# Two-layer graph kernel: short products gathered into blocks of two graphs, on five shared single PSUM banks

## The chip, the cores and the metric

The kernel runs on one core of one Trainium2 chip. The metric is the device time of one launch in microseconds (us), from the first to the last instruction of that core. Inputs and outputs lie in the chip's main memory, all in 32-bit floats.

A core has a tensor engine (PE, matrix products; its weight loads are listed as PEld), a vector engine (DVE), a scalar engine (ACT), GpSimd (POOL), and a queue engine (SP) that issues transfers (DMA). PE writes its results into PSUM, a small memory that is handed out in banks of 512 floats for each of 128 partitions; DVE and ACT read them from there.

## What is computed

There are 128 graphs of 128 nodes with 512 features each, and one adjacency matrix for all. Two layers follow each other, each with a residual sum and a normalization over the features:

```python
def layer0(x, adj, Wq, Wk, Wv):
    q, k, v = x @ Wq.T, x @ Wk.T, x @ Wv.T              # for each graph
    rel = adj.T * (q @ k.T)
    rel = rel / norm(rel, over the last axis)
    return rel @ v

def layer1(x, adj, Wq, bq, Wk, bk, Wv, bv):              # 8 heads of 64
    q, k, v = x @ Wq + bq, x @ Wk + bk, x @ Wv + bv      # split into heads
    scores = q @ k.T / sqrt(64) + where(adj == 0, -1e9, 0)
    return softmax(scores) @ v                           # heads side by side

x = layernorm(x + layer0(x, adj, ...))
x = layernorm(x + layer1(x, adj, ...))
```

## The kernel before

The graphs are worked on in 32 groups of four (`g`), with `b` the graph within its group. Layer 0 uses one folded matrix `m` for q and k. The five large products (m, v0, q, k, v1) are each done on four graphs at once, with seven half-size products in place of eight. Each of the seven is a dense step: 8 matmul instructions of 256 columns.

```python
def product(self, i, bank, start):
    ...
    for m in range(2):
        for k in range(2):
            nc.tensor.matmul(bank[:, m, :], l[:, k, m * P:(m + 1) * P], r[:, k, :], ...)

def step(self, i):
    if i == 1:
        self.begin()
        self.a = ps_a.tile([P, 2, HF], F32, tag="a", ...)
        self.product(1, self.a, True)
        self.empty(self.s[:, 0], self.a, 0)          # ACT empties the partial sum
    elif i == 5:
        self.b = ps_b.tile([P, 2, HF], F32, tag="b", ...)
        ...
    elif i == 2:
        d = ps_b.tile([P, 2, HF], F32, tag="d", ...)
        self.product(2, d, True)
        self.add(0, 0, d, 0)                         # DVE adds and empties
    elif i == 6:
        self.product(6, self.a, False)               # adds on to what is in the bank
        self.empty(self.s[:, 2], self.a, 0)
    # ... 3 and 7 add on to b and a and are added by DVE, 4 is emptied by ACT
```

Everything else is short work. The program of every engine is written by hand, by a table of positions. `at(r, k, f, ...)` puts a piece of short work into round `r` ahead of dense step `k`; a round has 35 positions, and a position over 35 falls into the next round. Halves give only a finer order: 10.5 and 11 both stand between the dense steps 10 and 11.

```python
R = 35
def at(r, k, f, *a):
    short.setdefault(R * r + k, []).append((f, a))

for r in range(-1, NG):
    todo = [("m", r + 1), ("v0", r + 1)] if r < NG - 1 else []
    ...
    todo += [("q", r), ("k", r), ("v1", r)]
    for j, (kind, g) in enumerate(todo):
        ...
        for k, i in ((0, 1), (1, 5), (3, 6), (4, 2), (5, 3), (6, 7), (9, 4)):
            dense[R * r + 7 * j + k] = (pr, i)
```

The short work on PE that matters here:

```python
def l0_score(g, b):                      # scores of layer 0, whole array
    p = ps_m.tile([P, P], F32, tag="m", name=f"pst_{g}_{b}")
    ...
def l0_norm(g):                          # sums of squares: 128 rows, 32 columns of the array
    pn = ps_m.tile([P, G, Q], F32, tag="m", name=f"pn_{g}")
    for q in range(A):
        nc.tensor.matmul(pn[q * Q:(q + 1) * Q], ones, sq[:, :, q * Q:(q + 1) * Q], ...)
    nc.vector.transpose(ss, pn)
    ...
def l0_out(g, b):                        # rel @ v of layer 0, whole array
    p = ps_m.tile([P, D], F32, tag="m", name=f"po0_{g}_{b}")
    ...
def attn_scores(g, b):                   # 8 heads, two side by side on 64 rows each
    p = ps_s.tile([P, 2, A, H // 2, Q], F32, tag="s", name=f"ps_{g}_{b}")
    for a in range(H // 2):
        for s in range(2):
            r = slice(s * HD, (s + 1) * HD)
            nc.tensor.matmul(p[:, s, :, a, :], QT[g][r, a, b, :], KT[g][r, a, b, :], start=True, stop=True)
    w = two.tile(...)
    nc.vector.scalar_tensor_tensor(w..., p..., HD ** -0.5, mask..., op0=ALU.mult, op1=ALU.add)
def attn_out(g, b):                      # 8 heads, two side by side on 64 columns each
    p = ps_m.tile([P, H // 2, P], F32, tag="m", name=f"po1_{g}_{b}")
    for a in range(H // 2):
        for s in range(2):
            h = 2 * a + s
            nc.tensor.matmul(p[s * HD:(s + 1) * HD, a, :], V1[g][:, b, h * HD:(h + 1) * HD],
                             wT[:, s * (H // 2) + a].rearrange("p q t -> p (q t)"), start=True, stop=True)
    oT = one.tile(...)
    nc.vector.transpose(oT..., p...)
    ...
```

Between the scores and the product with v of one graph stand the row maximum (DVE), eight exponentials (ACT), a write to main memory and back in another order (`attn_spill`, `attn_stage`), and a transpose in blocks of 32 (`attn_transpose`, DVE). After the product its transpose goes out and back once more (`attn_back`, `attn_rows`). `attn_sum` divides by the softmax's sums and adds bias and residual, and `attn_stats`, `attn_norm` and `attn_write` finish the graph.

The PSUM pools before, in banks: `ps_a` 2, `ps_b` 2 (tags b and d), `ps_s` 2 (one tile of two banks), `ps_m` 2.

Of the kernel before, what the change touches and what calls it, by code (L numbers as in the profile page):

```python
# [8 lines left out]
F32 = mybir.dt.float32  # L9
# [9 lines left out]
def kernel(  # L19
# [15 lines left out]
    nc = tc.nc  # L35
# [14 lines left out]
    dram = ctx.enter_context(tc.tile_pool(name="dram", bufs=2, space=bass.MemoryType.DRAM))  # L50
    ps_a = ctx.enter_context(tc.tile_pool(name="ps_a", bufs=2, space=bass.MemoryType.PSUM))
    ps_b = ctx.enter_context(tc.tile_pool(name="ps_b", bufs=1, space=bass.MemoryType.PSUM))
    ps_s = ctx.enter_context(tc.tile_pool(name="ps_s", bufs=1, space=bass.MemoryType.PSUM))
    ps_m = ctx.enter_context(tc.tile_pool(name="ps_m", bufs=2, space=bass.MemoryType.PSUM))

    Q = 32
    A = P // Q
# [185 lines left out]
    class Projection:  # L243
# [56 lines left out]
# [3 lines that stand above are left out]
                self.a = ps_a.tile([P, 2, HF], F32, tag="a", name=f"pa_{self.name}")  # L303
                self.product(1, self.a, True)
                self.empty(self.s[:, 0], self.a, 0)
            elif i == 5:
                self.b = ps_b.tile([P, 2, HF], F32, tag="b", name=f"pb_{self.name}")
                self.product(5, self.b, True)
                self.empty(self.s[:, 1], self.b, 1)
            elif i == 2:  # L310
                d = ps_b.tile([P, 2, HF], F32, tag="d", name=f"pd_{self.name}")
                self.product(2, d, True)
                self.add(0, 0, d, 0)
            elif i == 6:
                self.product(6, self.a, False)
                self.empty(self.s[:, 2], self.a, 0)
            elif i == 3:
                self.product(3, self.b, False)
                self.add(0, 1, self.b, 2)
            elif i == 7:  # L320
                self.product(7, self.a, False)
                self.add(1, 1, self.a, 1)
            elif i == 4:
                self.product(4, self.a, False)
                self.empty(self.out(1, 0), self.a, 1)
# [65 lines left out]

    def attn_scores(g, b):

        p = ps_s.tile([P, 2, A, H // 2, Q], F32, tag="s", name=f"ps_{g}_{b}")
        for a in range(H // 2):
            for s in range(2):
                r = slice(s * HD, (s + 1) * HD)
                nc.tensor.matmul(p[:, s, :, a, :], QT[g][r, a, b, :], KT[g][r, a, b, :], start=True, stop=True)  # L398

        w = two.tile([P, 2, A, H // 2, Q], F32, tag="xl" if g == NG - 2 and b >= 2 else "w", name=f"w_{g}_{b}")  # L400
        nc.vector.scalar_tensor_tensor(w.rearrange("p s q a r -> p s (q a r)"),  # L401
                                       p.rearrange("p s q a r -> p s (q a r)"), HD ** -0.5,
                                       mask[:, None, :].to_broadcast([P, 2, D]), op0=ALU.mult, op1=ALU.add)
        nmax = small.tile([P, H], F32, tag="nmax", name=f"nmax_{g}_{b}")
        sums = small.tile([P, H], F32, tag="sums", name=f"sums_{g}_{b}")
        SOFT[g, b] = [w, nmax, sums]
# [26 lines left out]
            nc.sync.dma_start(wl[q * Q:(q + 1) * Q].rearrange("p a i r -> p a (i r)"), rows[:, :, q, :])  # L433

    def attn_transpose(g, b):
        wT = one.tile([P, H, A, Q], F32, tag="wT", name=f"wT_{g}_{b}")
        nc.vector.transpose(wT, SOFT[g, b][0].rearrange("p a i r -> p i a r"))  # L437
        SOFT[g, b][0] = wT

# [2 lines left out]
    def attn_out(g, b):  # L442
# [4 lines left out]
        for a in range(H // 2):  # L447
            for s in range(2):
                h = 2 * a + s
                nc.tensor.matmul(p[s * HD:(s + 1) * HD, a, :], V1[g][:, b, h * HD:(h + 1) * HD],  # L450
                                 wT[:, s * (H // 2) + a].rearrange("p q t -> p (q t)"), start=True, stop=True)
        oT = one.tile([P, A, H // 2, Q], F32, tag="oT", name=f"oT_{g}_{b}")
        nc.vector.transpose(oT.rearrange("p q a r -> p a q r"), p.rearrange("p a (q t) -> p a q t", t=Q))  # L453
        rs = small.tile([P, 2, 2, H // 2], F32, tag="rs", name=f"rs_{g}_{b}")
        nc.vector.reciprocal(rs, sums.rearrange("p (s a) -> p s a", s=2)[:, :, None, :].to_broadcast([P, 2, 2, H // 2]))
# [16 lines left out]
    def attn_sum(g, b):  # L472

        o, xr, rs = SOFT[g, b]
        f = o.rearrange("p f a r -> p (f a) r")
        nc.vector.tensor_tensor(f, f, rs.rearrange("p s y a -> p (s y a)")[:, :, None].to_broadcast([P, A * H // 2, Q]),  # L476
                                op=ALU.mult)
        nc.gpsimd.tensor_tensor(xr, xr, bv_b, op=ALU.add)  # L478
        nc.gpsimd.tensor_tensor(o, o, xr.rearrange("p (a f r) -> p f a r", a=H // 2, f=A), op=ALU.add)  # L479
        SOFT[g, b] = o  # L480

    def attn_stats(g, b):
        o = SOFT.pop((g, b))
        stats = small.tile([P, 1, 2], F32, tag="stats1", name=f"st1_{g}_{b}")
        statistics(o.rearrange("p f a r -> p (f a r)"), stats, 0, f"1_{g}_{b}")
        rstd = inverse_std(stats, 1, f"1_{g}_{b}")
        SOFT[g, b] = o, rstd, shift(stats, rstd, 1, f"1_{g}_{b}")

    def attn_norm(g, b):
        o, rstd, sh = SOFT.pop((g, b))  # L490
        y = two.tile([P, D], F32, tag="y", name=f"y_{g}_{b}")
        nc.scalar.activation(y.rearrange("p (a f r) -> p f a r", a=H // 2, f=A), o, AF.Identity,
                             bias=sh[:, 0:1], scale=rstd[:, 0:1])
        SOFT[g, b] = y

    def attn_write(g, b):
        nc.sync.dma_start(out[g * G + b], SOFT.pop((g, b)))

# [4 lines left out]
            nc.gpsimd.tensor_tensor(X[g, h], X[g, h], bv_b[:, None, :].to_broadcast([P, 2, D]), op=ALU.add)  # L505

    def last_scores(g, b):
        p = ps_s.tile([P, 2, H // 2, P], F32, tag="s", name=f"ps_{g}_{b}")
        for a in range(H // 2):
            for s in range(2):  # L510
                r = slice(s * HD, (s + 1) * HD)
                nc.tensor.matmul(p[:, s, a, :], QT[g][r, a, b, :], KT[g][r, a, b, :], start=True, stop=True)
        w = two.tile([P, H, P], F32, tag="w" if b < 2 else "xl", name=f"w_{g}_{b}")
        nc.vector.scalar_tensor_tensor(w, p.rearrange("p s a j -> p (s a) j"), HD ** -0.5,
                                       maskp[:, None, :].to_broadcast([P, H, P]), op0=ALU.mult, op1=ALU.add)
        nmax = small.tile([P, H], F32, tag="nmax", name=f"nmax_{g}_{b}")
        nc.vector.tensor_reduce(nmax, w, axis=AX.X, op=ALU.max, negate=True)
        sums = small.tile([P, H], F32, tag="sums", name=f"sums_{g}_{b}")
        SOFT[g, b] = w, nmax, sums, graph(g, b)
# [15 lines left out]
    def last_out(g, b, s):  # L535

        _, _, sums, xr = SOFT[g, b]
        if s == 0:
            LT["p", b] = ps_b.tile([P, H // 2, 2, HD], F32, tag="bd"[b % 2], name=f"po1_{g}_{b}")
            LT["rs", b] = small.tile([P, H], F32, tag="rs", name=f"rs_{g}_{b}")  # L540
        if b == 0 and s == 0:
            LT["o"] = one.tile([P, G, D], F32, tag="v1", name=f"o_{g}")
# [30 lines left out]
    def last_store(g, b):  # L573
# [6 lines left out]
    R = 35  # L580
    dense, short = {}, {}

    QUICK = (
        (32, (34, 34, 34, 35), (36, 38), 38, (43, 44, 45, 47, 51, 51, 55.5, 56.5)),
        (35, (37, 38, 39, 40), (38, 40), 40, (46, 48, 48, 50, 53, 54, 56, 60)),
        (38, (40, 40.5, 40.5, 41), (42, 43), 46, (48, 51, 51, 52.5, 56.5, 59.5, 62, 62.5)),
        (38.5, (43, 44, 45, 45), (45, 47), 49, (52, 53, 54, 56, 60, 63, 65, 66)),
    )
    LAST = (
        (17, (19, 20), (24, 24), (25.5, 27), 31, 33, 33),  # L590
        (17.5, (20.5, 21.5), (24, 24.5), (25.5, 27.5), 34.5, 34.5, 35),
        (19, (24, 25), (27, 27), (28.5, 31.5), 34.5, 35.5, 36),
        (20.5, (23.5, 27), (30.5, 31), (34, 35), 38.5, 39, 39),
    )

    def at(r, k, f, *a):
# [14 lines left out]
    for g in range(NG):  # L611

        for h in range(2):
# [2 lines left out]
                at(g - 1, 12 + 4 * h, load, g, h)  # L616
        last = g == NG - 1

        sc, no, ou, de, ln, sp, st, tr = (
            (18, 22, (36, 36, 37, 37), 38, 39, 40, (42, 43), (46, 47, 49, 50)) if g == 0 else  # L620
            (11, 16, (18, 19, 21, 22), 23, 24, 25, (26, 28), (31, 32, 33, 34)) if last else
            (11, 17, (19, 21, 23, 25), 26, 27, 29, (30, 32), (36, 37, 39, 40)))
        for h in range(2):
            at(g - 1, sp + h * (g in (0, NG - 1)), x1_spill, g, h)
            at(g - 1, st[h], x1_stage, g, h)
        for i, (dh, h) in enumerate(halves):
            at(g - 2, ((24, 25, 27, 28) if g != 1 else (22, 23, 24, 25))[i], x_transpose, g, dh, h)
            at(g - 1, tr[i], x1_transpose, g, dh, h)
        for b in range(G):
            at(g - 1, sc + b, l0_score, g, b)  # L630
            at(g - 1, ou[b], l0_out, g, b)
            at(g - 1, ln + b // 2, l0_layernorm, g, b)
        at(g - 1, no, l0_norm, g)
        at(g - 1, de, l0_rstd, g)

# [2 lines left out]
        for b in range(G):  # L638
            if last:
# [7 lines left out]
                at(g, no, last_norm, g, b)  # L647
                at(g, w, last_store, g, b)
                continue
            if g == NG - 2:  # L650
                s, ex, sp, st, pk = QUICK[b]
            else:
                s = (32, 39, 46, 52)[b]
                v = s + (14, 13, 14, 15)[b]
                ex, sp, st = (s + 2, s + 3, s + 4, s + 5), (s + 4, s + 6), s + 8
                pk = v - 2, v, v + 1, v + 3, v + 6, v + 9 + (b == 1), v + 11 + (b == 1), v + 13
            at(g, s, attn_scores, g, b)
            at(g, s + 1, attn_max, g, b)
            for i in range(4):
                at(g, ex[i], attn_exp, g, b, 2 * i)  # L660
            for i in range(2):
                at(g, sp[i], attn_spill, g, b, i)
            at(g, st, attn_stage, g, b)
# [48 lines left out]
```

## Time and profile before

| | before |
|---|---|
| time, median of 3 | 2519.33 us (2519.09 to 2522.44) |
| span of the profiled run | 2520.1 us |
| instructions | 41502 |
| matmul instructions on PE | 14656 |
| masked scaling of the scores (DVE, 128x1024) | 124, 1211 ns each |
| transpose of the product with v (DVE, 128x512) | 124, 715 ns each |
| exponentials (ACT, 128x128) | 992, 392 ns each |
| additions into o (POOL, 128x512) | 124, 1271 ns each |
| traffic with main memory | 159 GB/s over the span |

How it is read: for each engine the profile gives the busy time and its share of the span, and for each group of instructions the count, the mean length of one, and the idle time ahead of them with what ended it. Names are those of the program's tiles: `pa`, `pb` and `pd` are the banks of dense steps, `ps` the scores of layer 1, `po<-wT,v` its product with v, `po<-v,rel` the product of layer 0, `pst` the scores of layer 0, `pn` the sums of squares. The column such as `64*128` gives the rows and columns of the array that a matmul uses. In the list of waits a line tells who waited for whom, for how long in total, how often, and the longest. A chain of waits is followed back from the last instruction. A timeline merges neighbours of one kind and gives start, length and count.

### The profile page before, as it was taken

What the parts mean: (1) busy time and instruction counts of PE and PEld (TensorE: products, weight loads), DVE (VectorE), ACT (ScalarE), POOL (GpSimd) and SP (SyncE); (2) the same over time, 40 slices, a digit from 0 to 9 for tenths busy, and PEclk for the clock granted to TensorE, in tenths of its full rate; (3) what the DMA queues carried; (4) which work ended last, traced back from release to release, by engine and by line L of the source; (5) the groups of instructions that cost most, each with busy time, mean ns of one, the idle gap of its engine ahead of it and who ended that gap; (6) DMA issues with size and microseconds to landing.
All of it is one profiled execution on the core that took longest, in us unless ns stands there. A gap on an engine that the chain in (4) does not pass through costs nothing.

```text
span 2520.1 us, 41502 instructions
## 1 busy us (share of the span) xinstructions
PE 2498.5 (99%) x14656; PEld 2105.4 (84%) x14656; DVE 1559.6 (62%) x2587; ACT 1020.4 (40%) x3211; POOL 840.5 (33%) x1206
## 2 busy tenths in 40 slices
PE   8999999999999999999999999999999999999998
PEld 5888888888888888888888888888888888888886
DVE  5455666655666656666556666666665666665667
ACT  1234344434444443444344444444443444433445
POOL 3223333333333233332333332333323333323333
PEclk9999999999999999999999999999999999999999
DMA  7356556656566565565655665656656556656554
GB/s 156 101 135 179 144 165 182 164 153 170 145 183 172 150 172 146 169 180 158 161 163 152 180 174 152 169 145 177 172 148 180 151 159 182 169 153 169 147 166 134
DMA packets 508561, 404.74 MB, mean 161 GB/s; under 512 B 37568, under 2 KB 424768, under 8 KB 508352
## 3 DMA queue, kind: packets, MB, share of 16 engines
q1 hardware_dynamic: 508352, 402.08, 59.1%
q8 instruction: 115, 1.88, 0.3%
q14 instruction: 94, 0.77, 0.1%
HBM read 237.31 MB, written 164.63 MB: 159 GB/s over the span
## 4 chain that ended last, share of the span: by engine, by line
PE 98%; DVE 1%; DMA 1%; issue 0%; POOL 0%; SPq 0%; POOLq 0%; ACT 0%; DVEq 0%
PE pa_v L283 17%; PE pa_q L283 9%; PE pa_m L283 9%; PE pa_k L283 9%; PE pb_v L283 9%; PE ps L398 5%; PE po L450 5%; PE pst L335 5%; PE po L380 5%; PE pd_v L283 5%; PE pb_q L283 4%; PE pb_k L283 4%; PE pb_m L283 4%; PE pd_m L283 2%; PE pd_k L283 2%; PE pd_q L283 2%
## 5 line engine op out<-in xcount | busy, mean ns | idle before, releaser
L418 ACT ACTIVATE w<-w,nmax 128x128 f32<-128x128 f32 x992 | 385.6, 392 | 441.1 <-DVE nmax L411 412.9
L283 PE MATMUL pa_v<-wc_v,tx 128*128 128x256 f32 x1536 | 363.2, 379 | 0.4 <-DVE v L298 0.4
L283 PEld LDWEIGHTS pa_v<-wc_v,tx 128*128 128x128 f32 x1536 | 289.2, 190 | 38.8 <-DVE v L298 0.6
L453 DVE STREAM_TRANSPOSE oT<-po 128x512 f32<-128x512 f32 x124 | 88.7, 715 | 331.6 <-PE po L450 331.6
L360 POOL TENSOR_SCALAR ve<-st 128x1 f32<-128x1 f32 (+1 forms) x160 | 36.5, 228 | 628.7 <-DVE st L356 625.7
L478 POOL TENSOR_TENSOR xr<-xr,bv_b 128x512 f32<-128x512 f32 x124 | 159.2, 1284 | 234.7 <-DMA xr<-x1d 213.8
L479 POOL TENSOR_TENSOR o<-o,xr 128x512 f32<-128x512 f32 x124 | 157.6, 1271 | 147.1 <-DVE o L476 136.4
L401 DVE SCALAR_TENSOR_TENSOR w<-ps,mask 128x1024 f32<-128x1024 f32 x124 | 150.2, 1211 | 69.1 <-PE ps L398 68.9
L337 POOL TENSOR_TENSOR sq<-rel 128x128 f32<-128x128 f32 x128 | 51.1, 399 | 421.4 <-DVE rel L336 421.4
L476 DVE TENSOR_TENSOR o<-o,rs 128x512 f32<-128x512 f32 x124 | 89.0, 718 | 164.2 <-DMA o<-od 164.2
L418 ACT ACTIVATION_READ_ACCUMULATOR w<-w,nmax 128x1 f32 x992 | 188.4, 190 | 0.0
L283 PE MATMUL pa_q<-tx,wc_q 128*128 128x256 f32 x768 | 184.9, 383 | 0.0
L283 PE MATMUL pa_m<-tx,wc_m 128*128 128x256 f32 x768 | 181.5, 379 | 0.8 <-DVE yT L298 0.8
L283 PE MATMUL pa_k<-tx,wc_k 128*128 128x256 f32 x768 | 181.6, 379 | 0.0
L283 PEld LDWEIGHTS pa_q<-tx,wc_q 128*128 128x128 f32 x768 | 143.2, 190 | 37.3 <-issue 15.0
L294 ACT ACTIVATE s_q<-pa_q,bq_sb 128x256 f32<-128x256 f32 x128 | 53.6, 469 | 274.9 <-PE pa_q L283 273.5
L283 PEld LDWEIGHTS pa_m<-tx,wc_m 128*128 128x128 f32 x768 | 145.8, 190 | 21.4 <-DVE yT L298 1.2
L283 PEld LDWEIGHTS pa_k<-tx,wc_k 128*128 128x128 f32 x768 | 145.8, 190 | 20.1 <-issue 0.2
L411 DVE TENSOR_REDUCE nmax<-w 128x4 f32<-128x512 f32 x248 | 156.4, 672 | 0.1
L375 ACT ACTIVATE x<-x,sh,rstd 128x512 f32<-128x512 f32 x128 | 93.9, 804 | 153.3 <-POOL sh L370 153.3
L437 DVE STREAM_TRANSPOSE wT<-wl 128x1024 f32<-128x1024 f32 x124 | 153.1, 1235 | 0.6 <-DMA wl<-wd 0.4
L398 PE MATMUL ps<-kT,qT 64*128 64x128 f32 x1984 | 144.1, 285 | 0.0
(159 smaller groups left out, 5036.0 us busy)
## 6 DMA issues: line engine op xcount, KB each, us to landing
wd<-w SPq DMA_DIRECT2D x248, 256.0 KB, 2.6
wl<-wd SPq DMA_DIRECT2D x496, 128.0 KB, 3.0
xl_x<-in_x_dram SPq DMA_DIRECT2D x256, 128.0 KB, 6.7
x<-in_x_dram SPq DMA_DIRECT2D x64, 512.0 KB, 5.9
x1d<-x SPq DMA_DIRECT2D x64, 512.0 KB, 2.8
xl_h<-x1d SPq DMA_DIRECT2D x256, 128.0 KB, 3.5
od<-oT SPq DMA_DIRECT2D x496, 64.0 KB, 1.8
o<-od SPq DMA_DIRECT2D x124, 256.0 KB, 3.1
```

What stands on the lines that cost most here:

```text
L283: nc.tensor.matmul(bank[:, m, :], l[:, k, m * P:(m + 1) * P], r[:, k, :], start=start and m == 0 and k == 0, stop=(m == 1 and k == 1), ski ...
L335: nc.tensor.matmul(p, XT[g][:, dc, b, :], YT[g][:, dc, b, :], start=(dc == 0), stop=(dc == C - 1))
L375: nc.scalar.activation(h, h, AF.Identity, bias=sh[:, b:b + 1], scale=rstd[:, b:b + 1])
L380: nc.tensor.matmul(p, REL[g][0][:, b, :], V0[g][:, b, :], start=True, stop=True)
L398: nc.tensor.matmul(p[:, s, :, a, :], QT[g][r, a, b, :], KT[g][r, a, b, :], start=True, stop=True)
L401: nc.vector.scalar_tensor_tensor(w.rearrange("p s q a r -> p s (q a r)"), p.rearrange("p s q a r -> p s (q a r)"), HD ** -0.5, mask[:, Non ...
L411: nc.vector.tensor_reduce(nmax[:, s * (H // 2):(s + 1) * (H // 2)], w[:, s].rearrange("p q a r -> p a q r"), axis=AX.XY, op=ALU.max, negat ...
L418: nc.scalar.activation(w[:, s, :, a, :], w[:, s, :, a, :], AF.Exp, bias=nmax[:, i:i + 1], accum_out=sums[:, i:i + 1])
L437: nc.vector.transpose(wT, SOFT[g, b][0].rearrange("p a i r -> p i a r"))
L450: nc.tensor.matmul(p[s * HD:(s + 1) * HD, a, :], V1[g][:, b, h * HD:(h + 1) * HD], wT[:, s * (H // 2) + a].rearrange("p q t -> p (q t)"), ...
L478: nc.gpsimd.tensor_tensor(xr, xr, bv_b, op=ALU.add)
L479: nc.gpsimd.tensor_tensor(o, o, xr.rearrange("p (a f r) -> p f a r", a=H // 2, f=A), op=ALU.add)
```

## The change

The change moves the short work of layer 1 on PE. Before, the four graphs of a group have their scores at positions 32, 39, 46 and 52 and their products with v at 46, 52, 60 and 67, each graph for itself. After it, the scores of graphs 0 and 1 stand at 32 and those of graphs 2 and 3 at 51; the products with v of graphs 0 and 1 stand at 51 too, those of graphs 2 and 3 at 67, which is position 32 of the next round. So products of two graphs and scores of two others follow one another without a dense step between. The positions of the rest of the short work are set anew in tables, layer 0's included; the dense steps stay as they are.

To hold several short products at once, all of them share one pool of five single banks: the scores take two single banks instead of one double, and the masked scaling is one instruction for each. The `pd` bank of the dense steps comes from this pool too. So that two graphs can be under way, `wT` and `oT` get two buffers. Room for them is made by leaving out the tile `y`: the last sum is written to x1's own tile `xr`, normalized in place and stored from there.

```diff
     ps_b = ctx.enter_context(tc.tile_pool(name="ps_b", bufs=1, space=bass.MemoryType.PSUM))
-    ps_s = ctx.enter_context(tc.tile_pool(name="ps_s", bufs=1, space=bass.MemoryType.PSUM))
-    ps_m = ctx.enter_context(tc.tile_pool(name="ps_m", bufs=2, space=bass.MemoryType.PSUM))
+    ps_m = ctx.enter_context(tc.tile_pool(name="ps_m", bufs=5, space=bass.MemoryType.PSUM))
...
-                d = ps_b.tile([P, 2, HF], F32, tag="d", name=f"pd_{self.name}")
+                d = ps_m.tile([P, 2, HF], F32, tag="m", name=f"pd_{self.name}")
...
     def attn_scores(g, b):
-        p = ps_s.tile([P, 2, A, H // 2, Q], F32, tag="s", name=f"ps_{g}_{b}")
+        p = [ps_m.tile([P, A, H // 2, Q], F32, tag="m", name=f"ps_{g}_{b}_{s}") for s in range(2)]
         for a in range(H // 2):
             for s in range(2):
                 r = slice(s * HD, (s + 1) * HD)
-                nc.tensor.matmul(p[:, s, :, a, :], QT[g][r, a, b, :], KT[g][r, a, b, :], start=True, stop=True)
+                nc.tensor.matmul(p[s][:, :, a, :], QT[g][r, a, b, :], KT[g][r, a, b, :], start=True, stop=True)
...
-        nc.vector.scalar_tensor_tensor(w.rearrange("p s q a r -> p s (q a r)"),
-                                       p.rearrange("p s q a r -> p s (q a r)"), HD ** -0.5,
-                                       mask[:, None, :].to_broadcast([P, 2, D]), op0=ALU.mult, op1=ALU.add)
+        for s in range(2):
+            nc.vector.scalar_tensor_tensor(w[:, s].rearrange("p q a r -> p (q a r)"),
+                                           p[s].rearrange("p q a r -> p (q a r)"), HD ** -0.5, mask,
+                                           op0=ALU.mult, op1=ALU.add)
...
-        wT = one.tile([P, H, A, Q], F32, tag="wT", name=f"wT_{g}_{b}")
+        wT = two.tile([P, H, A, Q], F32, tag="wT", name=f"wT_{g}_{b}")
...
-        oT = one.tile([P, A, H // 2, Q], F32, tag="oT", name=f"oT_{g}_{b}")
+        oT = two.tile([P, A, H // 2, Q], F32, tag="oT", name=f"oT_{g}_{b}")
...
-        nc.gpsimd.tensor_tensor(o, o, xr.rearrange("p (a f r) -> p f a r", a=H // 2, f=A), op=ALU.add)
-        SOFT[g, b] = o
+        xr_ = xr.rearrange("p (a f r) -> p f a r", a=H // 2, f=A)
+        nc.gpsimd.tensor_tensor(xr_, xr_, o, op=ALU.add)
+        SOFT[g, b] = xr
...
     def attn_norm(g, b):
-        o, rstd, sh = SOFT.pop((g, b))
-        y = two.tile([P, D], F32, tag="y", name=f"y_{g}_{b}")
-        nc.scalar.activation(y.rearrange("p (a f r) -> p f a r", a=H // 2, f=A), o, AF.Identity,
-                             bias=sh[:, 0:1], scale=rstd[:, 0:1])
-        SOFT[g, b] = y
+        normalized(SOFT[g, b][0], 0, *SOFT[g, b][1:])
```

The last group's scores and products get the same kind of banks. The tables of the steady groups, in the order scores, (maximum, four pairs of exponentials), (two spills), stage, (transpose, product with v, back, rows, sum, statistics, normalization, write), for the four graphs:

```diff
+    STEADY = (
+        (32, (35.5, 35.5, 35.5, 35.5, 36), (35.5, 36), 39, (41.5, 51, 52, 53.5, 56.5, 59.5, 59.5, 61.5)),
+        (32, (33.5, 37.5, 39, 41.5, 41.5), (42, 42), 42, (50, 51, 54.5, 60, 60.5, 63, 65.5, 72)),
+        (51, (51.5, 51.5, 51.5, 53.5, 53.5), (52, 53.5), 56, (60, 67, 67, 68, 72, 74.5, 78, 78)),
+        (51, (53, 54, 56, 56.5, 56.5), (56, 59), 61, (64.5, 67, 67.5, 74, 77, 81, 82, 84)),
+    )
...
-                s = (32, 39, 46, 52)[b]
-                v = s + (14, 13, 14, 15)[b]
-                ex, sp, st = (s + 2, s + 3, s + 4, s + 5), (s + 4, s + 6), s + 8
-                pk = v - 2, v, v + 1, v + 3, v + 6, v + 9 + (b == 1), v + 11 + (b == 1), v + 13
+            s, ex, sp, st, pk = QUICK[b] if g == NG - 2 else STEADY[b]
```

Layer 0's work in the steady rounds, in the order scores, norm, products, inverse deviation, normalization, spills, stages, transposes:

```diff
-            (11, 17, (19, 21, 23, 25), 26, 27, 29, (30, 32), (36, 37, 39, 40)))      # scores at 11 to 14
+        ((10.5, 14, 10.5, 14), 15.5, (22, 22, 20.5, 18.5), 22.5, (24.5, 27), (32, 29.5), (33.5, 29.5), (36.5, 40.5, 41, 43.5)),
```

Two more tables, `QUICK` for the last group but one and `LAST` for the last, are set anew in the same manner. In `QUICK` the scores move from 32, 35, 38 and 38.5 to 31.5, 35.5, 36 and 40.5.

## The prediction

> **What bounds the kernel now.** I read the page first, then the list of the tensor engine's waits, then its timeline over one round in the steady middle. The page gives busy shares and the chain that ended last:
>
> ```profile
> PE 2498.5 (99%) x14656; PEld 2105.4 (84%) x14656; DVE 1559.6 (62%) x2587; ACT 1020.4 (40%) x3211; POOL 840.5 (33%) x1206
> ...
> PE 98%; DVE 1%; DMA 1%; issue 0%; POOL 0%; SPq 0%; POOLq 0%; ACT 0%; DVEq 0%
> ```
>
> PE is busy for 99% of the span and makes up 98% of the chain; the vector engine has 38% to spare. PE's two longest waits, of about a dozen microseconds in all, are for data:
>
> ```profile
> PE pM L178 <- DMA wk_s<-in_L_gnn_Wk_dram: 4.3, 1, 4.3
> PE pa_v L283 <- DVE xT L197: 2.3, 1, 2.3
> ```
>
> Both are at the start. The count of each is one, so none of the 31 rounds waits for anything. Only PE's own time can be shortened, and a busy PE record is not PE at its peak (the page says that ends are modelled). So I looked at starts. The timeline of PE (start, length, line, tiles, count) around one lone score group, and around one product with v that is followed by scores:
>
> ```profile
> 1059.01 1.89 PE L283 MATMUL pa_m<-tx,wc_m 128*128 128x256 f32 x8
> 1060.83 1.16 PE L398 MATMUL ps<-kT,qT 64*128 64x128 f32 x16
> 1061.92 1.99 PE L283 MATMUL pd_m<-xT,wc_m 128*128 128x256 f32 x8
> 1063.75 1.89 PE L283 MATMUL pb_m<-xT,wc_m 128*128 128x256 f32 x8
> ```
>
> ```profile
> 1044.61 1.89 PE L283 MATMUL pa_v<-wc_v,tx 128*128 128x256 f32 x8
> 1046.43 1.09 PE L450 MATMUL po<-wT,v 128*64 128x128 f32 x16
> 1047.45 1.16 PE L398 MATMUL ps<-kT,qT 64*128 64x128 f32 x16
> 1048.54 1.99 PE L283 MATMUL pd_v<-wc_v,x1T 128*128 128x256 f32 x8
> 1050.38 1.89 PE L283 MATMUL pb_v<-wc_v,x1T 128*128 128x256 f32 x8
> ```
>
> A projection step between others takes 1.727 us from start to start (median of the trace's record starts). The one ahead of a short group takes 1.82, the one behind it 1.83. The groups on half arrays (the column 64\*128 or 128\*64) are also longer than their content. To see that, I cut the timeline's window inside the two groups:
>
> ```profile
> 1013.20 0.55 PE L450 MATMUL po<-wT,v 128*64 128x128 f32 x6
> ...
> 1013.20 0.99 PE L450 MATMUL po<-wT,v 128*64 128x128 f32 x14
> ```
>
> ```profile
> 1014.23 0.60 PE L398 MATMUL ps<-kT,qT 64*128 64x128 f32 x6
> ...
> 1014.23 1.05 PE L398 MATMUL ps<-kT,qT 64*128 64x128 f32 x14
> ```
>
> Eight more matmuls, four pairs that run side by side, take 0.44 us for po and 0.45 us for ps: 0.11 and 0.112 us a pair. Eight pairs are 0.876 us (po) and 0.896 us (ps) by the unrounded starts. What a block takes beyond that is the price of changing the array's tiling:
>
> - lone ps: 0.093 (step ahead) + 1.092 + 0.104 (step behind) = 1.289 us, of it 0.896 content, 0.393 price;
> - lone po, likewise: 0.093 + 1.024 + 0.105 = 1.222 us, price 0.346;
> - po then ps: 0.093 + 1.024 + 1.092 + 0.104 = 2.313 us, content 1.772, price 0.541.
>
> The single starts say where it sits: the first start of a tiled group comes 309 ns after the last dense one instead of 216, the second pair 153 ns (po) or 207 (ps) after the first pair instead of 103 to 105; the next group starts 202 ns after the last pair, and its own second matmul comes about 104 ns late.
>
> **What the Trainium skill says.** "TensorEngine Tiling (Array Packing)", section Key Properties: "Mode switching requires drain", that is, a change of tiling mode, not of the tile within a mode, drains the engine. The trace agrees: some 0.1 us at each side of each border, none between the pairs inside a group. "TensorE: Matmul & The Clock Gate", section The mechanism, lets a weight load run beside a matmul in flight only where the row groups differ. Here weight loads run beside matmuls in the dense steps too (PEld 84% of the span beside PE's 99%), so I don't use it. "PSUM — Partial Sum Buffer", section Specifications, gives 8 banks of 2 KiB a partition. The pools before and after both come to 8 such banks, which the trace can't show.
>
> **The change, part by part.**
>
> *Blocks.* From the tables, a steady round before has tiled work ahead of steps 4 (ps), 11 (po, ps), 17 (po, ps, pn), 25 (po) and 32 (po, ps): three pairs, one lone ps, one lone po, and pn (0.356 us more, behind ps). That is 3 x 2.313 + 1.289 + 1.222 + 0.356 = 9.81 us. After, there are two blocks, ahead of 16 (pn, po, po, ps, ps) and 32 (po, po, ps, ps). If a second group of the same tiling costs its content alone, each is 2.313 + 0.876 + 0.896 = 4.085 us; with pn's 0.356 the two are 8.53 us. The round loses 1.28 us. Check of the bookkeeping: 35 steps x 1.727 + layer 0's scores and products (4 x 0.891 + 4 x 0.858) + 9.81 = 77.25 us, and the trace repeats at 984.74 and 1061.99, 77.25 apart. So a round becomes 75.97 us.
>
> Thirty groups of graphs (0 to 29) use the steady tables: 30 x 1.28 = 38.4 us. Group 30 and the last group have about one block fewer between them (scores of graphs 1 and 2 now stand together): 0.4 us. Together 38.8 us, all of it on PE, which is the path.
>
> *Five banks.* Scores take two single banks where they took one double one. The masked scaling becomes two instructions: 1.211 us for 1024 columns today; the same operation on 512 columns from PSUM takes 0.750 us (x<-po,rn,x), and other 512-wide ones 0.69. I take 1.4 us for the two, 0.2 more, x 128 graphs = 25 us of DVE, 62% to 63% of the span, beside PE: nothing on the path.
>
> *x1's tile takes the sum.* One POOL addition of 1.27 us as before, with the other operand's order; the normalization in place takes ACT's 0.804 us (x<-x) instead of 0.814 (y<-o). Both engines are under half busy: nothing. It frees y's room for a second wT and oT, which two neighbouring products need.
>
> *Start and end.* The first rounds' tables for layer 0 are unchanged. In the last 25 us PE waits in five places, 3.4 us in sum, for DVE or ACT; five banks and a new order may take some of it back, the longer DVE work gives some away. I put -0.5 us, a guess.
>
> Sum: 2519.3 - 38.8 - 0.5 = **2480 us**, 1.6% less.
>
> **Rivals.**
>
> *A wait for a bank.* A block of four wants six banks and has five, seven with pn. The last score group needs the banks of pn and of the first po. From the block's start: pn 0.36, first po done at about 1.5 (with the 0.27 us a matmul takes to end), its transpose on DVE 0.715 us, so free at about 2.3. The last scores start at 0.36 + 1.80 + 0.20 + 0.90 = 3.3. A spare of 1 us, if DVE isn't behind; ahead of it stand only two products by adj (0.286 each) and one wT transpose (1.235), placed one or two steps of 1.7 us earlier. For the block without pn the spare is about the same. If DVE is behind after all, I reckon 0.3 us a block, 60 blocks: 18 us back, 2498 us.
>
> *Work in bursts.* Two graphs' exponentials now come together: 16 of them, with a spacing of 0.385 us in the trace's ACT timeline, are 6.2 us in a row at worst, and ACT must also empty a partial sum within two steps (3.4 us). The table spreads them in groups of 2 to 8: at step 0 eight (3.1 us) stand between the emptying of step 0's bank and that of step 1's; the bank of step 1 is needed again by step 5, three steps (5.2 us) after step 1 ends. Likewise pn follows layer 0's last score by two steps (3.5 us), where adj product 0.286 and square 0.399 are to be done; before it had over 7 us. If one such wait of 0.5 us comes each round, 15 us are lost: 2495.
>
> *The border stays.* If two po of different graphs cost a drain at their seam too, because the weights are new and the bank is another, four seams a round keep 0.1 to 0.2 us: up to 0.8 of the 1.28 us is gone and the time is about 2504. Against: inside a group each pair already loads new weights, at an even 0.11 us.
>
> *Nothing at all, or worse.* That would take over a microsecond of new waits each round. All the data chains got longer distances (scores to product with v: 16 to 19 steps instead of 13 to 15), which speaks against it.
>
> **Range and chances.** The count of borders is firm and their prices vary by a nanosecond or so in the trace; all the doubt is in new waits, which only lengthen, and in the end (a few us either way). Hence 2473 to 2494, longer above than below. Faster by over 2% means under 2469, which needs 11 us that I can't find: 0.05. Slower by over 2% needs 90 us of waits: 0.02. The rest, 0.93, is within 2%.
>
> **What would show it.** Right: rounds of 75.97 us; two tiled blocks a round, 4.09 and 4.44 us with the edges of their dense neighbours; the second po starting 0.11 us after the last pair of the first, the second ps likewise; the list of PE's waits as short as now; about 128 x 2 masked scalings of 0.7 us. Wrong: a wait of ps for DVE's oT or w in the list (bank rival), of pa or pb for ACT's s, or pn for sq (bursts), or a gap of 0.2 us between the two po (border rival). A round of 77 us without waits would mean that the mode isn't what costs.

## The result and the profile after

The changed kernel takes 2481.89 us (median of 4 runs, 2480.21 to 2482.69) against 2519.79 us of the kernel before beside it. The ratio is 0.9847, with a 95% interval of 0.983 to 0.9864: 37.9 us less, 1.5%. The prediction said 2480.

The page of the changed kernel, busy shares and the chain that ended last:

```profile
PE 2461.6 (99%) x14656; PEld 2115.2 (85%) x14656; DVE 1603.6 (65%) x2715; ACT 1012.8 (41%) x3211; POOL 833.5 (34%) x1206
...
PE 98%; DVE 1%; issue 0%; DMA 0%; POOL 0%; POOLq 0%; ACT 0%; SPq 0%; DVEq 0%
```

The number of matmuls is the same, their busy time 36.9 us less, and PE still makes up 98% of the chain. The same work got shorter; no wait in the rounds went away, as there was none. PE's list of waits has, as before, only a few events near the start and the end; two of its lines:

```profile
PE pM L177 <- DMA wk_s<-in_L_gnn_Wk_dram: 4.4, 1, 4.4
PE po L546 <- DVE o L551: 1.8, 3, 1.2
```

PE's timeline around one block shows two groups of one tiling merged into one line of 32 matmuls:

```profile
1027.17 1.89 PE L282 MATMUL pa_v<-wc_v,tx 128*128 128x256 f32 x8
1028.99 1.97 PE L450 MATMUL po<-wT,v 128*64 128x128 f32 x32
1030.89 2.06 PE L397 MATMUL ps<-kT,qT 64*128 64x128 f32 x32
1032.87 2.00 PE L282 MATMUL pd_v<-wc_v,x1T 128*128 128x256 f32 x8
1034.70 1.89 PE L282 MATMUL pb_v<-wc_v,x1T 128*128 128x256 f32 x8
```

From 1027.17 to 1034.70 are 7.53 us; less two dense steps of 1.727 the block takes 4.08 us, and the prediction had 4.085. In the trace's starts the second po begins 103 ns after the last matmul of the first, as every pair inside a group does, and the second ps 105 ns after the first. In all 60 blocks it is 101 to 104 and 104 to 106 ns: the seam, the place where two groups of one tiling meet, is free. The block with pn:

```profile
1067.63 1.89 PE L282 MATMUL pb_q<-tx,wc_q 128*128 128x256 f32 x8
1069.45 0.43 PE L345 MATMUL pn<-sq,ones 128*32 128x128 f32 x8
1069.81 1.97 PE L450 MATMUL po<-wT,v 128*64 128x128 f32 x32
1071.70 2.06 PE L397 MATMUL ps<-kT,qT 64*128 64x128 f32 x32
1073.69 2.00 PE L282 MATMUL pa_v<-wc_v,tx 128*128 128x256 f32 x8
1075.52 1.89 PE L282 MATMUL pa_q<-tx,wc_q 128*128 128x256 f32 x8
```

It takes 7.89 - 3.45 = 4.44 us. A round (from one `pd_m<-xT` step to the same step of the next round) takes 75.956 us in all 29 rounds that can be compared so, against 77.246: 1.290 less. 29 x 1.290 = 37.4 us of the 39.5 by which the two profiled spans differ. The stretch ahead of those rounds is 1.4 us shorter. Of this, 0.3 us is the order's (the round ahead of them takes 70.18 us instead of 70.47, and 70.47 again with the old tables below); the other 1.1 us is scatter of the start, as the end of this stretch lies anywhere between 131.9 and 137.2 us in the experiments below (134.9 and 133.6 in these two). The stretch behind gave 1.0 us up to the last dense step and took back 0.3 after it. So 37.4 + 0.3 + 1.0 = 38.7 us can be put down to the order, where the prediction had 38.8.

### The profile page after: what moved, and what is told of

It reads as the page before. It is cut to its first block, busy times and chain, and to the rows that moved or that the text cites. A ratio compares the mean times of both kernels' runs of the same rounds, so it can differ in the third digit from the quotient of the medians.

```text
span 2480.6 us, 41595 instructions
## 1 busy us (share of the span) xinstructions
PE 2461.6 (99%) x14656; PEld 2115.2 (85%) x14656; DVE 1603.6 (65%) x2715; ACT 1012.8 (41%) x3211; POOL 833.5 (34%) x1206
## 4 chain that ended last, share of the span: by engine, by line
PE 98%; DVE 1%; issue 0%; DMA 0%; POOL 0%; POOLq 0%; ACT 0%; SPq 0%; DVEq 0%
PE pa_v L282 18%; PE pa_m L282 9%; PE pa_q L282 9%; PE pa_k L282 9%; PE pb_v L282 9%; PE ps L397 5%; PE po L450 5%; PE pd_v L282 5%; PE pst L334 5%; PE po L379 4%; PE pb_q L282 4%; PE pb_k L282 4%; PE pb_m L282 4%; PE pd_q L282 2%; PE pd_k L282 2%; PE pd_m L282 2%
## 5 line engine op out<-in xcount | busy, mean ns | idle before, releaser
L478 POOL TENSOR_TENSOR xr<-xr,bv_b 128x512 f32<-128x512 f32 x124 | 164.7, 1328 | 709.5 <-DMA xr<-x1d 300.6
L480 POOL TENSOR_TENSOR xr<-xr,o 128x512 f32<-128x512 f32 x124 | 157.4, 1269 | 288.6 <-issue 267.8
L418 ACT ACTIVATION_READ_ACCUMULATOR w<-w,nmax 128x1 f32 x992 | 193.6, 195 | 0.0
L290 ACT COPY s_m<-pa_m 128x512 f32<-128x512 f32 x64 | 37.1, 580 | 330.6 <-PE pa_m L282 320.1
L290 ACT COPY s_v<-pa_v 128x512 f32<-128x512 f32 x128 | 74.9, 585 | 233.7 <-PE pa_v L282 233.7
L401 DVE SCALAR_TENSOR_TENSOR w<-ps,mask 128x512 f32<-128x512 f32 x248 | 154.2, 684 | 24.2 <-PE ps L397 24.2
L374 ACT ACTIVATE xr<-xr,sh,rstd 128x512 f32<-128x512 f32 x124 | 100.8, 813 | 128.6 <-POOL sh L369 128.6
L196 DVE STREAM_TRANSPOSE x1T<-xl_h 128x512 f32<-128x512 f32 x128 | 90.1, 704 | 72.7 <-DMA xl_h<-x1d 72.7
L334 PEld LDWEIGHTS pst<-yT,xT 128*128 128x128 f32 x1024 | 124.7, 192 | 3.7 <-ACT yT L290 0.4
L397 PE MATMUL ps<-kT,qT 64*128 64x128 f32 x1984 | 127.7, 279 | 0.0
```

Of the source, the lines that this page charges most:

```text
L290: nc.scalar.copy(dst, bank)
L334: nc.tensor.matmul(p, XT[g][:, dc, b, :], YT[g][:, dc, b, :], start=(dc == 0), stop=(dc == C - 1))
L374: nc.scalar.activation(h, h, AF.Identity, bias=sh[:, b:b + 1], scale=rstd[:, b:b + 1])
L397: nc.tensor.matmul(p[s][:, :, a, :], QT[g][r, a, b, :], KT[g][r, a, b, :], start=True, stop=True)
L401: nc.vector.scalar_tensor_tensor(w[:, s].rearrange("p q a r -> p (q a r)"), p[s].rearrange("p q a r -> p (q a r)"), HD ** -0.5, mask, op0= ...
L418: nc.scalar.activation(w[:, s, :, a, :], w[:, s, :, a, :], AF.Exp, bias=nmax[:, i:i + 1], accum_out=sums[:, i:i + 1])
```

## Experiments

My theory: each change of PE's tiling has a price, and the gain is the number of changes saved, times it. The rivals: the banks, the tile or the dense borders give it; or the price stays at each seam.

**The steady tables of before, all else changed.** In `STEADY` and in layer 0's line of `ZERO`:

```diff
-        (32, (35.5, 35.5, 35.5, 35.5, 36), (35.5, 36), 39, (41.5, 51, 52, ...)),
-        (32, ...), (51, ...), (51, ...)
+        (32, (33, 34, 35, 36, 37), (36, 38), 40, (44, 46, 47, 49, 52, 55, 57, 59)),
+        (39, ...), (46, ...), (52, ...)
```

> The changed kernel with the steady tables of before (groups 0 to 29, layer 0's too); the five banks, the split scaling, x1's tile and the two last tables stay. My theory (the price of changing the tiling, nothing else): the rounds go back to 77.25 us and the time to about 2519 us, with no waits of PE in the rounds. Rival (the banks, or x1's tile, gave part of it): rounds clearly under 77.25, a time of 2485 to 2510 us. Second rival (the split scaling costs PE something): over 2525 us.

Measured: 2520.17 us, ratio to the kernel before 1.0 (0.9992 to 1.0009), rounds of 77.247 us. The five banks, the split scaling, the second buffers, x1's tile and the two last tables are worth nothing by themselves and cost PE nothing. All of the gain sits in the order of the steady rounds. (Whether that order needs the second buffers was not tried; the banks are tried below.)

**Two lone pieces joined to blocks.** From the experiment above, two moves:

```diff
-        (39, (40, 41, 42, 43, 44), ...),                                # scores of graph 1
+        (32, (40, 41, 42, 43, 44), ...),
-        (46, ..., (58, 60, 61, 63, 66, 69, 71, 73)),                    # graph 2: its product with v at 60
+        (46, ..., (58, 67, 68, 69, 72, 75, 77, 79)),
```

> As the old tables, with two pieces moved: the scores of graph 1 from 39 to 32 and the product with v of graph 2 from 60 to 67, so that the lone score group and the lone product of a round join blocks that are there. My theory: a round loses the two lone prices, 0.393 + 0.346 = 0.74 us, so 76.5 us, and 30 rounds lose 22 us: about 2497 us. Pieces without a wait ahead: the list of PE's waits stays short. Rival (a second group of one tiling pays at the seam too, 0.1 to 0.2 us): 76.7 to 76.9 us a round, 2503 to 2509 us.

Measured: 2498.69 us, ratio 0.9916 (0.9901 to 0.993), rounds of 76.502 us: 0.745 less, where the two lone prices add up to 0.74. So more than half of the change's gain comes from two moves, and the seam is free here too. The rest of the way to the changed kernel, 76.502 - 75.956 = 0.546 us, joins two pairs of product and scores into one block, which saves the price of one pair, 0.541 us by the prediction. Layer 0's positions change on this way too, but its pieces take the same time from start to start in both kernels (scores 0.89 us, products 0.86). The joined block in PE's timeline:

```profile
1034.71 1.97 PE L450 MATMUL po<-wT,v 128*64 128x128 f32 x32
1036.61 2.06 PE L397 MATMUL ps<-kT,qT 64*128 64x128 f32 x32
```

Its 1.90 us from po to ps are those of the changed kernel.

**Another order inside the blocks.** Fractions of a position order the pieces; all four stay between the same two dense steps. The positions in words:

```diff
-    product with v of 0 at 51, of 1 at 51, scores of 2 at 51, of 3 at 51
+    product with v of 0 at 50.6, scores of 2 at 50.7, product with v of 1 at 50.8, scores of 3 at 50.9
-    product with v of 2 at 67, of 3 at 67, scores of 0 at 32, of 1 at 32
+    product with v of 2 at 66.6, scores of 0 at 31.7, product with v of 3 at 66.8, scores of 1 at 31.9
```

> The changed kernel with another order inside the blocks: product, scores, product, scores in place of product, product, scores, scores. Same work, same places among the dense steps. My theory (each change of the tiling costs): a block gets one more change each way, 0.147 (ps to po) + 0.201 (po to ps) = 0.35 us, 60 blocks: 21 us, about 2503 us, rounds of 76.65 us. Rival (what costs is to leave and enter the dense steps, as when partial sums are handed over): no difference, 2482 us. Second rival (order eases or worsens the waits for banks): a wait of ps or po in PE's list.

Measured: 2501.0 us, ratio 0.9925 (0.9911 to 0.994), rounds of 76.654 us, 0.698 over the changed kernel: 0.349 a block, the price of the two added changes to a nanosecond. No dense border was added, and PE's list of waits stays as short as before, so neither rival holds. The timeline:

```profile
1036.62 1.09 PE L450 MATMUL po<-wT,v 128*64 128x128 f32 x16
1037.64 1.16 PE L397 MATMUL ps<-kT,qT 64*128 64x128 f32 x16
1038.73 1.09 PE L450 MATMUL po<-wT,v 128*64 128x128 f32 x16
1039.76 1.16 PE L397 MATMUL ps<-kT,qT 64*128 64x128 f32 x16
1040.85 1.99 PE L282 MATMUL pd_v<-wc_v,x1T 128*128 128x256 f32 x8
```

From po to the dense step are 4.23 us; in the changed kernel it was 3.88.

**One dense step in between.** The products of graphs 2 and 3 go one step ahead:

```diff
-        ..., (52, 53.5), 56, (60, 67, 67, ...)
-        ..., (56, 59), 61, (64.5, 67, 67.5, ...)
+        ..., (52, 53.5), 56, (60, 66, 67, ...)
+        ..., (56, 59), 61, (64.5, 66, 67.5, ...)
```

> The changed kernel with the products with v of graphs 2 and 3 one dense step earlier (66 in place of 67), so that one dense step stands between them and the scores in one of the two blocks of a round. My theory: one more exit and entry in place of one change from po to ps, 0.204 + 0.195 - 0.201 = 0.20 us a round, rounds of 76.15 us and a time of about 2488 us. Rival (the drain at a dense border is hidden by the dense step's weight loads when it has a step of its own): 75.96 us a round, 2482 us.

Measured: 2487.89 us, ratio 0.9879 (0.9863 to 0.9896), rounds of 76.153 us: 0.197 more. The trace holds the figure that the bare times would leave doubtful. The dense step alone between two tilings costs both edges:

```profile
1027.70 1.97 PE L450 MATMUL po<-wT,v 128*64 128x128 f32 x32
1029.60 1.99 PE L282 MATMUL pa_v<-wc_v,tx 128*128 128x256 f32 x8
1031.52 2.06 PE L397 MATMUL ps<-kT,qT 64*128 64x128 f32 x32
```

It takes 1.92 us (1.924 by the unrounded starts), 0.197 over a dense step among others.

The next three ask what the banks are for.

**The pools of before under the new tables.**

```diff
-    ps_m = ...(name="ps_m", bufs=5, ...)
+    ps_s = ...(name="ps_s", bufs=1, ...)          # one tile of two banks for scores
+    ps_m = ...(name="ps_m", bufs=2, ...)
-    d = ps_m.tile(..., tag="m", ...)
+    d = ps_b.tile(..., tag="d", ...)              # and the scores' tile, their scaling and the last group's tiles as before
```

> The changed kernel's tables with the pools of before: one double bank for scores, emptied by one instruction of 1.22 us, two single banks for the other short products, one for pd. My theory (the banks bring nothing themselves, but the blocks can't do without them): in each block the second score group has to wait until the first is scaled. By the changed kernel's vector timeline that scaling would start 3.09 us after the block's first product and end 1.22 later, some 1.5 us after the second group could have started: 60 blocks x 1.5 = 90 us, about 2572 us, slower than the kernel before, with ps waiting for DVE's w some 60 times in PE's list. Rival (the vector engine's slack hides it): 2482 us.

Measured: 2578.82 us, ratio 1.023 (1.0215 to 1.0245): slower than the kernel before. The list of PE's waits and the timeline of one block:

```profile
PE ps L398 <- DVE w L401: 81.0, 61, 1.3
```

```profile
1067.75 1.16 PE L398 MATMUL ps<-kT,qT 64*128 64x128 f32 x16
1070.23 1.16 PE L398 MATMUL ps<-kT,qT 64*128 64x128 f32 x16 [1.33 <-DVE w L401]
1071.33 1.99 PE L283 MATMUL pd_v<-wc_v,x1T 128*128 128x256 f32 x8
```

The second scores start 2.49 us after the first (the unrounded starts). In the changed kernel it is 0.995, so they are 1.49 late, as worked out ahead; the list has only 1.33, as the modelled length of the matmul ahead covers the rest. And the round is 79.148 us, 3.19 more than the changed kernel's: 1.60 a block. The wait costs 0.1 us more than the delay, as the group behind it starts anew: its second pair comes 207 ns after the first instead of 105, as when a group is entered from another tiling, and it takes 1.09 us to the dense step (unrounded) where 0.99 would do.

**Four banks.** In the pool `ps_m`, `bufs=5` becomes `bufs=4`.

> The changed kernel with four shared banks instead of five. My theory: the last score group of a block then needs the bank of the second product; its transpose ends 0.15 us before that group's start, and the scaling of the first scores ends about as the next dense step needs its bank. So no wait or at most 0.1 us a block: 2482 to 2488 us. Rival (the five banks are what the gain rests on, each of them): over 2500 us.

Measured: 2482.42 us, ratio 0.9849 (0.9833 to 0.9865), rounds of 75.956 us, no wait added to the rounds. The fifth bank isn't needed.

**Three banks.** `bufs=3`.

> The changed kernel with three shared banks. My theory: the last half of a block's scores then needs the bank of the first half of the first scores, whose scaling ends about 1.0 us after that group could start: 60 x 1.0 = 60 us, about 2542 us, with ps waiting for DVE's w about 60 times, 1 us each. Rival (banks go round fast enough at any number from three): below 2500 us. Second rival (waits for banks add up beyond the block, with pd and layer 0's products): over 2570 us.

Measured: 2546.6 us, ratio 1.0103 (1.0088 to 1.0118), rounds of 78.033 us: 2.08 more, 1.04 a block, as the bank's release was worked out. The list shows less than that:

```profile
PE ps L397 <- DVE w L401: 34.2, 61, 0.6
```

```profile
1054.43 1.38 PE L397 MATMUL ps<-kT,qT 64*128 64x128 f32 x18
1056.37 1.16 PE L397 MATMUL ps<-kT,qT 64*128 64x128 f32 x14 [0.56 <-DVE w L401]
1057.46 1.99 PE L282 MATMUL pd_v<-wc_v,x1T 128*128 128x256 f32 x8
```

The group of 18 is the reason: one half's first matmul of the second scores (two instructions) starts alone, as its bank is free, and its modelled length covers part of the time in which the other half waits. The other half starts 0.94 us late by the trace's starts, and 0.10 for the start anew come on top. From 1054.43 to 1057.46 are 3.03 us, against 1.99 in the changed kernel. The 1.04 is read from starts, not from the idle column.

## Why the prediction was right

**The bound** held: PE without waits in the rounds before and after. In all seven experiments the changed kernel's time plus thirty times the difference of the rounds gives the measured time within 2.4 us.

**The price of the tiling** was the right cause. The prediction's sum gave 1.28 us a round; measured 1.290. The experiments give the single terms back: 0.745 for two lone prices (worked out 0.739), 0.349 for a change each way (0.348), 0.197 for an exit and an entry in place of one change (0.198). The old tables with the new banks, at ratio 1.0, close the account. Nor is it a price of any short piece between dense steps. Layer 0's scores, on the whole array, leave their neighbours as they are:

```profile
1055.42 1.89 PE L282 MATMUL pa_v<-wc_v,tx 128*128 128x256 f32 x8
1057.15 1.95 PE L334 MATMUL pst<-yT,xT 128*128 128x128 f32 x16
1058.93 1.89 PE L282 MATMUL pd_v<-wc_v,xT 128*128 128x256 f32 x8
1060.66 1.89 PE L282 MATMUL pb_v<-wc_v,xT 128*128 128x256 f32 x8
```

The dense steps ahead of and behind pst take 1.73 us from start to start; beside a tiled group they take 1.82 and 1.83. One reading of the prediction was too narrow: it set aside the section The mechanism of the Trainium skill's page "TensorE: Matmul & The Clock Gate". The same section also lets a weight load run ahead into a background weight buffer, so the loads beside the matmuls of the dense steps don't contradict it as a whole. Nothing here rests on it.

**The seam** between two graphs of one tiling was the step that could not be seen before, only argued from the pairs inside a group. It is free: 103 and 105 ns, new weights and another bank included. The rival of the border that stays is out.

**The bank rival** did not come true. The vector engine's timeline of the changed kernel in the block with pn, which starts at 1069.45:

```profile
1069.94 0.32 DVE L347 STREAM_TRANSPOSE ss<-pn 128x128 f32<-128x128 f32 x1 [2.40 <-PE pn L345]
1070.95 0.72 DVE L453 STREAM_TRANSPOSE oT<-po 128x512 f32<-128x512 f32 x1 [0.69 <-PE po L450]
```

The bank of the first po is free at 1071.67, 2.22 us after the block's start (worked out: 2.3). The last scores start 0.995 after 1071.70, at 3.25 (worked out: 3.3). DVE is idle ahead of that transpose, not behind. The spare of 1 us was real, and larger than needed: with four banks the rounds have no wait, with three each block loses 1.04 us.

**The bursts** cost PE nothing, as reckoned: pn, `pa` and `pb` wait for nobody in the rounds.

**Terms that were off** are small. For start and end I put -0.5 us as a guess. From the last dense step's start to the end it is 25.29 us against 24.96, but in the experiments with the same last tables and banks it lies between 24.48 and 25.74, so this guess is neither confirmed nor refuted. Two scalings take 2 x 0.684 = 1.37 us (said: 1.4). DVE's busy time grew by 44 us, not 25: the longer records of the scaling are 19.5 of it (248 x 0.684 less 124 x 1.211), and 17.5 come from `tx<-x1T,tx` (see below), which I hadn't looked at; the rest was not worked out. The normalization in place takes 0.813 us, not 0.804. None of these lies on the path. The median fell by 37.9 us where the sum said 39.3; the difference is inside the ratio's interval.

## What to carry to other kernels

Where PE is full and nothing waits, look at the starts: a group whose spacing at its edges is wider than inside may pay for a change of tiling, and then such groups should follow one another by kind, also from different iterations. Count the changes before and after, times the price from the trace, and the gain can be estimated ahead, here to 0.01 us a round. Then work out for each bank when it is free again and when it is wanted next: here the pools of before cost 1.60 us a block under the new order, a shared pool of four was enough, a fifth bank gave nothing more, and with three the waits lost more than the order gained.

## What the runs showed that I had not expected

A wait in the midst of a tiled block cost about 0.1 us beyond the delay, for the start anew (1.49 us late, 1.60 us lost). So the late second pair, a part of the price, comes after a stop too, without any change of tiling. And where one half of a pair can start, the list of waits hides part of the loss: 0.56 us listed of 1.04.

The vector engine's subtraction into tx takes 0.69 us in the kernel before and, with the same operands, 1.29 us in the changed one, in 29 of 32 cases. The kernel before, and the changed one:

```profile
1066.55 0.69 DVE L208 TENSOR_TENSOR tx<-x1T,tx 128x512 f32<-128x512 f32 x1
```

```profile
1054.99 1.26 POOL L480 TENSOR_TENSOR xr<-xr,o 128x512 f32<-128x512 f32 x1 [3.03 <-issue]
1055.51 1.29 DVE L207 TENSOR_TENSOR tx<-x1T,tx 128x512 f32<-128x512 f32 x1
```

It now starts while GpSimd adds to xr. The Trainium skill, "SBUF — State Buffer", section Who interferes with whom, says that a vector instruction with two operands in SBUF contends with a GpSimd instruction that reads there. The traces agree. Over all nine of them the 174 subtractions that start during this addition take 1.29 to 1.30 us and end about 0.55 us after it; the 114 others take 0.69, among them all of the two experiments that have the same addition but the old tables or only two moves. In the kernel before, another addition of GpSimd (`tx<-x1T`) starts 0.1 us after the subtraction and leaves it at 0.69, so it seems to matter which of the two starts first. No run moved this subtraction alone. As PE waits for nobody in the rounds, it cost nothing.
